# Two graph layers on one Trainium2 core: the order of work between layer 0 and the attention

## The chip, the cores and the metric

The kernel runs on one core of a Trainium2 chip. The metric is device time in microseconds (us) from start to end of one execution; three runs of the kernel before took 2220.85 to 2221.81, median 2221.29. A core has TensorE (matrix products), VectorE, ScalarE and GpSimd (called POOL in the profile), SyncE (SP), which issues most transfers, and DMA engines that carry them between the memory and the core. Each engine works through its own list of instructions in order, and instructions of different engines wait for each other where data or a buffer demands it.

## The reference

There are 3327 nodes with 1024 features, and an adjacency with about 1% of its entries filled. Layer 0 multiplies the adjacency with quantised features; layer 1 is an attention with 8 heads of 64, followed by a small network, each added to its input.

```python
# layer 0
h = relu(layernorm(x))
x = x + output            # adj @ support_q, scaled; support_q from h and the quantised weight
# layer 1
h = relu(layernorm(x))
Wh = einsum('nf,hfd->hnd', h, W)
e_src = einsum('hnd,hd->hn', Wh, a1); e_dst = einsum('hnd,hd->hn', Wh, a2)
e = leaky_relu(e_src[:, :, None] + e_dst[:, None, :], 0.2)
att = softmax(where(adj > 0, e, NEG))
h = elu(att @ Wh)         # heads side by side, then
x = x + mlp(h)            # 512 -> 256 -> 256 -> 512 -> 1024
```

The softmax is not computed entry by entry. The exponential of the leaky unit is one of two products, exp(src) exp(dst) or the same with slope 0.2, and which one holds depends on whether src > -dst. So the kernel keeps, for each node and head, its features times both exponentials ("features") and their difference, and multiplies them with two 0/1 matrices: the adjacency, and the adjacency where src > -dst.

## The kernel before

The nodes are padded to 26 tiles of 128 (`T = 26`). Each tile of columns is also a step `j` of the sums.

**Layer 0, second product (lines 711 to 757).** For each tile `t`, 104 products with 512 columns run in four parts (`SUBS`: 7, 6, 7 and 6 values of `j`), each `j` with an upper and a lower half of the adjacency (`hi`, `lo`) against `s_int[j]`. Then y is scaled on ScalarE and VectorE (L742, L744), added to the input (L745), written to `x1_d`, normalised (`normalised`, L137) and its inverse deviation `r` is formed (`half_inverse`: a root on ScalarE, reciprocals on VectorE). `transposed_by_dma` turns y: two copies on ScalarE (`yh`), two transposing transfers on SyncE's list (`yht`), two copies into `ht`. The last tile is turned by TensorE instead (`transposed_by_tensor`, two groups of four, both through one bank of `last_ps`).

**Heads (L630).** `heads(t)` forms Wh for a tile: eight products of `ht` with `whead` into `whm` (16 matmuls in the profile), then `wht` on ScalarE (called `taken`), on VectorE two products and two reductions for src and dst, the exponentials on ScalarE, two scalings `ft` on VectorE, and an upper half `fw` (ScalarE) and lower half `lows` (VectorE). POOL writes them to `feat_d` and `dsum_d` in memory. The src values are collected, turned by TensorE (`sp`) in the tiles named in `BATCHES` (12, 23 and 25) and written to `src_d` in rows. Heads of tile t - 1 stand before the last part of tile t's products; the last tile's stand after the loop, with `own` naming two tiles in the core (`f_even`, `dw`) that receive its values directly.

**Attention (L789 on).** `attends` has 32 entries of a half of the nodes, a head and one of two groups of row tiles. Each has 26 steps `n`. A step takes one selection `sel` on VectorE (L1057: one tile of columns for 7 or 6 row tiles, from `srow`, `ndst` and `mask`) and 7 or 6 products `acc` with `f_even` or `f_odd` (L1071). The four buffers of `sel` let VectorE run four steps ahead. In between stand products with the whole adjacency, called edges (L852, `mps<-dw,mf`): `mf` is the mask as numbers, cast on ScalarE in two halves, and `dw` the differences of features. `edge_steps(n)` says how many of them are due before step n: none until `FIRST`, then 12 a step up to `START` = 24, from `YOUNG` on in equal shares up to 338 at `LATE` = 62.

**The order around the change.** Order is written out by pins: `issue_after(a)` puts what is issued in its block behind `a` on the same engine, `queue_behind(a, b)` puts `a` behind `b`, without a wait of their own. Attention takes the memory of layer 0: `mask0` lies where `s_int` 0 to 6 were, `f_even` and `dw` where 6 to 19 were, `mask1` where 19 to 23 were, and each load waits until these were used last. SyncE's list before is: the transpositions of tile 24's y (`turned` is the second), xt of tile 25, `srow`, the first halves of seven masks, `f_even` for tiles 0 to 6, the masks' second halves, `f_even` and `dw` to tile 19, six masks of `mask1`, then `young`: `f_even` and `dw` for tiles 20 to 23, and for tile 24; `f_odd` after them. Steps 0 to 3 of the attention run while tile 25 is normalised, each of steps 4 to 11 ahead of one of the last heads' products.

Of the kernel before, what the change touches and what calls it, by code (L numbers as in the profile page):

```python
# [8 lines left out]
F32 = mybir.dt.float32  # L9
# [6 lines left out]
ALU = mybir.AluOpType  # L16
# [28 lines left out]
PARTS = SUBS  # L45
BATCHES = {12: 0, T - 3: 13, T - 1: T - 2}
GT = 2
# [14 lines left out]
def two_layer_kernel(  # L62
# [105 lines left out]
    with tc.tile_pool(name="at", bufs=2, reuse_waits="tile") as atp:  # L168
# [419 lines left out]
        with tc.tile_pool(name="wh", bufs=1, reuse_waits="tile") as whp, tc.tile_pool(  # L588
# [30 lines left out]

            def transposed_by_tensor(y):  # L620
                ht = s2.tile([P, KF, P], F32, name="ht", bufs=1)
                for g in range(KF // 4):
                    tp = last_ps.tile([P, 4, P], F32, tag="last", name="tp2")
                    for q in range(4):
                        k = 4 * g + q
                        nc.tensor.transpose(tp[:, q, :], y[:, k * P : (k + 1) * P], ident)
                    last = nc.scalar.copy(ht[:, 4 * g : 4 * g + 4, :], tp)
                return ht, last

            def heads(t, ht, r, own=None):  # L630
                if t == T - 1:
                    whm, sp = (last_ps.tile([P, EMB], F32, tag="last", name=n) for n in ("whm", "sp"))
                else:
                    whm = wh_ps.tile([P, EMB], F32, name="whm")
                    sp = sp_ps.tile([P, EMB], F32, name="sp")
                of_k, products = [], []
                for k in range(KF):
# [7 lines left out]
                ins = taken = nc.scalar.activation(wht, whm, AF.Copy, scale=r)  # L645
                if t < T - 1:
                    tc.keep_in_program_order(ins)
# [8 lines left out]
                nc.vector.tensor_scalar(ndst[:, t], dst, -1.0, None, ALU.mult)  # L656
                nc.scalar.activation(ratio[:, t], src, AF.Exp, scale=1.0 - SLOPE)
                if t in BATCHES:
                    first = BATCHES[t]
# [5 lines left out]
                    nc.scalar.copy(srct[:n], sp[:n, :P])  # L665
                    for u in range(first, t + 1):
                        d, sub = next((d, sub) for d, sub in zip(src_d, SUBS) if u in sub)
                        nc.gpsimd.dma_start(
                            d[:, (u - sub[0]) * P : (u - sub[0] + 1) * P],
                            srct[(u - first) * NH : (u - first + 1) * NH],  # L670
                        )

                ft = s2.tile([P, NH, 2, HC], F32, name="ft", bufs=1)
                wh3 = wht.rearrange("p (h d) -> p h d", d=HD)
                for q, slope in enumerate((1.0, SLOPE)):
                    exps = nc.scalar.activation(ft[:, :, q, HD], dst, AF.Exp, scale=slope)
                    scaled = nc.vector.tensor_tensor(  # L677
                        ft[:, :, q, :HD], wh3, ft[:, :, q, HD:].to_broadcast([P, NH, HD]), ALU.mult
                    )
                fw = s2.tile([P, NH, 2, 2 * HC], F32R, name="fw", bufs=1)  # L680
                f2 = ft.rearrange("p h q c -> p h (q c)")
                if own is not None:

                    parts = [dst[:, t].rearrange("p (q c) -> p q c", q=2) for dst in own]
                    ups = parts[0][:, 0], parts[1][:, 0].rearrange("p (e c) -> p e c", e=2)
                    downs = parts[0][:, 1], parts[1][:, 1].rearrange("p (e c) -> p e c", e=2)
                    values = f2[:, 0], ft[:, :2, 1]
                    for up, value in zip(ups, values):
                        nc.scalar.copy(up, value)
                    for up, down, value in zip(ups, downs, values):  # L690
                        scaled = nc.vector.tensor_tensor(down, value, up.bitcast(F32), ALU.subtract)
                nc.scalar.copy(fw[:, :, 0], f2)
# [15 lines left out]
                )  # L708
                return of_k, products, lows, exps, scaled, taken

            before = None
            for t in range(T):
# [27 lines left out]
                y = s2.tile([P, F], F32, name="y", bufs=1)  # L740
                with tc.issue_after(exps.ins) if t == T - 1 else nullcontext():
                    nc.scalar.activation(y, mm, AF.Copy, scale=r_asf)  # L742
                with tc.issue_after(made.ins) if t == T - 1 else nullcontext():
                    nc.vector.tensor_scalar(y, y, asf_t, sup_delta, ALU.mult, ALU.mult)  # L744
                nc.vector.tensor_tensor(xt, xt, y, ALU.add)  # L745
                nc.gpsimd.dma_start(x1_d[t * P : (t + 1) * P, :], xt)
                ln, v = normalised(y, xt)
                if t < T - 1:
                    ht, turned = transposed_by_dma(y)
                else:  # L750
                    ht, copied = transposed_by_tensor(y)

                with tc.issue_after(copied.ins) if t == T - 1 else nullcontext():
                    r = half_inverse(v, "ln")
                nc.vector.tensor_scalar(r, r, 2.0, None, ALU.mult)
                before = t, ht, r
            queue_behind(lows, ln)
            supp.close()
# [22 lines left out]
    EDGE = 13 * T  # L781
    FIRST = 12
    START = T - 2
    YOUNG = 14
    FRONT = 6
# [3 lines left out]
    with tc.tile_pool(name="srow0", bufs=1, reuse_waits="tile") as srow0, tc.tile_pool(  # L789
# [32 lines left out]
        def all_edges():  # L822

            for u, (c, g) in enumerate(units):
# [13 lines left out]
                for i in range(len(blocks)):  # L838
# [4 lines left out]
                    for j in range(T):  # L843
                        if j % TH == 0:
                            mf = (mf1 if j else mf0).tile([P, TH, P], F32R, tag="mf", name="mf")

                            amid = u == i == 0
                            with tc.issue_after(copied.ins) if amid else nullcontext():
                                ins = nc.scalar.copy(mf, mask[:, j : j + TH, :])  # L849
                            if amid:  # L850
                                queue_behind(taken, ins)
                        nc.tensor.matmul(ps, mf[:, j % TH, :], dw[:, j, :], start=(j == 0), stop=(j == T - 1))  # L852
                        if j == T - 1:
# [22 lines left out]

        mds = []
        edges = all_edges()
# [62 lines left out]

        old, young = PARTS[:3], [range(20, 24), range(24, 25)]
        with tc.issue_after(turned.ins):
            srow, ins = load_src(0)
        with tc.issue_after(ins.ins):
            ins = load_mask(0, SUBS[0], slice(0, TH))
        with tc.issue_after(ins.ins):
            load_features(f_even, feat_d, 0, old[:1])
            ins = load_mask(0, SUBS[0], slice(TH, T))
        with tc.issue_after(ins.ins):  # L950
# [3 lines left out]
            for js in young:  # L954
                load_features(f_even, feat_d, 0, [js])
                load_features(dw, dsum_d, 0, [js])
            load_features(f_odd, feat_d, 1, old + young + [range(T - 1, T)])
        for i, (c, g, e, si) in enumerate(attends):
# [82 lines left out]
            for j in range(T):  # L1041
# [12 lines left out]

                ahead = ln if j < 14 else scaled
                with tc.issue_after(ahead.ins) if i == 0 and j >= 4 else nullcontext():
                    ins = nc.vector.scalar_tensor_tensor(  # L1057
# [7 lines left out]
                if i == 0 and j < 4:  # L1065
                    queue_behind(products[0], ins)

                k = j - 4 if i == 0 and 4 <= j < 4 + KF else None
                with tc.issue_after(last_heads[k - 1].ins) if k else nullcontext():
                    for b in range(nb):  # L1070
                        ins = nc.tensor.matmul(  # L1071
                            accs[b], sel[:, b, :], f[:, j, :], start=(j == 0), stop=(j == T - 1)
                        )
# [126 lines left out]
```

## Time and profile before

| what | value |
|---|---|
| median of three runs | 2221.29 us |
| profiled execution, its own time | 2221.79 us |
| its span, first to last instruction | 2219.9 us |
| granted clock of TensorE, mean | 0.999 |
| last part of tile 25's products | 907.9 to 913.7 us |
| y of tile 25 normalised (L144 ends) | 920.0 us |
| heads' products of tile 25 | 923.2 to 935.6 us, between steps of attention |
| selection of step 14, first after tile 25's heads | 942.1 us |
| first attend ended (its sums copied) | 965.3 us on |

Times inside the kernel are given from the start of the span. A line of the timeline has start, duration, engine, line of the kernel, operation, what it writes and reads, the count of instructions merged, and in brackets how long the engine was idle before and what released it. One product with 512 columns appears as one instruction for layer 0 and as two for the heads. Durations of matmuls overlap; their spacing is what counts. The table of stretches gives, for each stretch, the busy time of each engine, then the granted clock, the mean share of the DMA engines and the data moved.

### The profile page before, as it was taken

To read this page: it belongs to the slowest core of one execution; us is meant where nothing else is said; L and a number is where in the kernel's file an instruction comes from. 1 tells how busy PE (TensorE), PEld (TensorE's weight loads), DVE (VectorE), ACT (ScalarE), POOL (GpSimd) and SP (SyncE) were. 2 spreads that over 40 slices of the span, in tenths; PEclk is the share of its full clock that TensorE was granted. 3 is DMA by queue.
4 is the path that set the end of the run, shared out by engine and by line. 5 is a ranking of instruction groups with operands and counts; after the bars stand their busy time and mean duration, and the time that the engine had idled before them with its cause. 6 is when DMAs were issued, how large, how long until landed. Compare 5 with 4: busy or idle time off the path is not lost.

```text
span 2219.9 us, 31285 instructions
## 1 busy us (share of the span) xinstructions
PE 2178.6 (98%) x12457; PEld 1748.6 (79%) x12457; DVE 1540.6 (69%) x1998; ACT 1113.6 (50%) x1714; POOL 176.0 (8%) x269
## 2 busy tenths in 40 slices
PE   5999999999999999999999999999999999999998
PEld 2477777777777777699999999999999999744444
DVE  8745555555455555678999999999999999732211
ACT  6734444544445544466555565555655555531220
POOL 2301000002000012000000000000000000000000
PEclk9999999999999999999999999999999999999999
DMA  6654566655655555934242422644242422383211
GB/s 218 164 185 155 158 189 181 179 165 156 183 184 184 170 168 157 331 116 149 87 149 78 142 90 73 222 143 149 83 149 87 140 87 78 102 208 114 104 57 57
DMA packets 242721, 321.40 MB, mean 145 GB/s; under 512 B 104900, under 2 KB 187284, under 8 KB 242576
## 3 DMA queue, kind: packets, MB, share of 16 engines
q1 hardware_dynamic: 222024, 246.24, 36.5%
q0 software_dynamic: 20544, 73.18, 10.5%
q8 instruction: 97, 1.59, 0.3%
q14 instruction: 48, 0.39, 0.1%
q10 hardware_dynamic: 8, 0.00, 0.0%
HBM read 208.99 MB, written 86.79 MB: 133 GB/s over the span
## 4 chain that ended last, share of the span: by engine, by line
PE 56%; DVE 1%; ACT 1%; issue 0%; DMA 0%; DVEq 0%
PE acc L1071 29%; PE mps L852 15%; PE o L1144 8%; PE h_ps L1107 4%; ACT enct L1129 0%; PE h_ps L1021 0%; PE whm L638 0%; DMA weights<-in_w1t 0%; DVE sel L1057 0%; ACT h L1114 0%; DVE nodes L1140 0%; DVE prod L652 0%; ACT su L896 0%; DVE ft L677 0%; DVE stats L141 0%
## 5 line engine op out<-in xcount | busy, mean ns | idle before, releaser
L1057 DVE SCALAR_TENSOR_TENSOR sel<-srow,ndst,mask 128x896 fp32r<-128x896 f32 (+1 forms) x832 | 864.8, 1082 | 52.3 <-PE acc L1071 40.1
L852 PE MATMUL mps<-dw,mf 128*128 128x260 f32 x2704 | 453.0, 283 | 0.3 <-ACT srct L665 0.3
L726 PE MATMUL mm<-s_int,hi 128*128 128x512 f32 x1352 | 426.7, 397 | 0.0
L726 PE MATMUL mm<-s_int,lo 128*128 128x512 f32 x1352 | 416.5, 389 | 0.0
L1071 PE MATMUL acc<-f_even,sel 128*128 128x260 f32 x2704 | 400.8, 286 | 3.1 <-DVE sel L1057 2.1
L1071 PE MATMUL acc<-f_odd,sel 128*128 128x260 f32 x2704 | 393.7, 286 | 1.1 <-ACT xs L1088 1.0
L849 ACT CAST mf<-mask 128x1664 fp32r<-128x1664 uint8 x208 | 331.4, 1594 | 118.8 <-PE mps L852 95.2
L852 PEld LDWEIGHTS mps<-dw,mf 128*128 128x128 f32 x2704 | 377.4, 188 | 1.1 <-ACT srct L665 0.6
L1071 PEld LDWEIGHTS acc<-f_even,sel 128*128 128x128 f32 x2704 | 356.8, 189 | 10.1 <-issue 3.6
L1071 PEld LDWEIGHTS acc<-f_odd,sel 128*128 128x128 f32 x2704 | 352.6, 188 | 8.4 <-issue 2.6
L726 PEld LDWEIGHTS mm<-s_int,hi 128*128 128x128 f32 x1352 | 254.0, 188 | 62.8 <-issue 12.0
L726 PEld LDWEIGHTS mm<-s_int,lo 128*128 128x128 f32 x1352 | 253.8, 188 | 52.7
L189 DVE TENSOR_TENSOR lo<-at,hi 128x896 fp32r<-128x896 f32 x104 | 106.2, 1021 | 132.4 <-ACT hi L185 132.2
L638 PE MATMUL whm<-whead,ht 128*128 128x512 f32 x416 | 183.8, 592 | 0.0
L1144 PE MATMUL o<-weights,h 128*128 128x512 f32 x416 | 179.7, 592 | 0.0
L190 DVE TENSOR_SCALAR mk<-at 128x896 uint8<-128x896 f32 (+1 forms) x104 | 61.5, 593 | 142.1 <-DMA at<-in_adj_t 142.1
L185 ACT CAST hi<-at 128x896 fp32r<-128x896 f32 x104 | 92.2, 886 | 135.4 <-PE mm L726 93.8
L1144 PEld LDWEIGHTS o<-weights,h 128*128 128x128 f32 x416 | 79.0, 190 | 99.1 <-issue 98.8
L638 PEld LDWEIGHTS whm<-whead,ht 128*128 128x128 f32 x416 | 78.3, 189 | 85.7 <-issue 83.8
L856 ACT COPY part<-mps 128x260 f32<-128x260 f32 x104 | 39.3, 378 | 188.2 <-PE mps L852 188.1
L1114 ACT ACTIVATE h<-h_ps,rest 128x512 f32<-128x512 f32 (+1 forms) x54 | 35.1, 653 | 194.2 <-PE h_ps L1107 194.2
L921 POOL DMA_DIRECT2D enc_d<-eh x64 | 57.5, 903 | 935.4 <-ACT eh L919 934.9
(166 smaller groups left out, 1666.6 us busy)
## 6 DMA issues: line engine op xcount, KB each, us to landing
feat_d<-fw POOLq DMA_DIRECT2D x26, 1040.0 KB, 5.3
f_even<-feat_d SPq DMA_DIRECT2D x7, 3380.0 KB, 13.5
f_odd<-feat_d SPq DMA_DIRECT2D x7, 3380.0 KB, 13.2
at<-in_adj_t SPq DMA_DIRECT2D x52, 448.0 KB, 4.3
at<-in_adj_t SPq DMA_DIRECT2D x52, 384.0 KB, 4.1
dw<-dsum_d SPq DMA_DIRECT2D x16, 910.0 KB, 9.0
dsum_d<-dw POOLq DMA_DIRECT2D x26, 520.0 KB, 6.3
x_d<-xt POOLq DMA_DIRECT2D x26, 512.0 KB, 6.7
```

The lines of the kernel that those rows point to most:

```text
L185: ins = nc.scalar.copy(hi, at)
L189: nc.vector.tensor_tensor(lo, at, hi.bitcast(F32), ALU.subtract)
L190: ins = nc.vector.tensor_scalar(mk[:, r], at, 0.0, None, ALU.is_gt)
L638: ins = nc.tensor.matmul(whm, ht[:, k, :], whead[:, k, :], start=(k == 0), stop=(k == KF - 1))
L726: nc.tensor.matmul(mm[:, c * 512 : (c + 1) * 512], which[:, q, :], s_int[j][:, c * 512 : (c + 1) * 512], start=(j == 0 and which is hi), s ...
L849: ins = nc.scalar.copy(mf, mask[:, j : j + TH, :])
L852: nc.tensor.matmul(ps, mf[:, j % TH, :], dw[:, j, :], start=(j == 0), stop=(j == T - 1))
L921: nc.gpsimd.dma_start(enc_d[q, sub[0] * P : (sub[-1] + 1) * P, h * HD : (h + 1) * HD].rearrange("(b p) d -> p b d", p=P), eh[:, q].rearran ...
L1057: ins = nc.vector.scalar_tensor_tensor(sel[:, :nb], srow[:, :nb], ndst[:, j, h : h + 1], mask[:, :, j, :], ALU.is_gt, ALU.mult,)
L1071: ins = nc.tensor.matmul(accs[b], sel[:, b, :], f[:, j, :], start=(j == 0), stop=(j == T - 1))
L1107: nc.tensor.matmul(ps[:, :cols], wt[:, k, m * P : (m + 1) * P], xt[:, k, :cols], start=(k == 0), stop=(k == k_n - 1),)
L1144: nc.tensor.matmul(ps[:, c * 512 : (c + 1) * 512], h3[:, k, q * P : (q + 1) * P], w4[:, k, c * 512 : (c + 1) * 512], start=(k == 0), stop= ...
```

## The change

- Tile 25 leaves `BATCHES`. The src values of tiles 24 and 25 are no longer turned; POOL writes each, 128 x 8 single numbers, straight to its places in `src_d`.
- `heads(24)` no longer stands before the last part of tile 25's products but behind them all, and stores its values also directly in `f_even` and `dw` (`own`). The loads of these for tile 24 are gone; `f_odd` loads tiles 24 and 25 one by one.
- `taken` and the first product of `heads(24)` stand behind the last operation of tile 25's deviation (`lacking`). The transpositions of tile 25 stand behind the products of `heads(24)`, the copies behind its `taken`, its exponentials behind the copies.
- Attention's step 0 stands between the two groups of transpositions, steps 1 to 3 between them and the heads of tile 25, steps 4 to 7 behind those heads, then 24 edges at once (`FIRST` 7, `YOUNG` 9), and step 8 behind them.
- On VectorE, selections 0 to 3 stand ahead of tile 25's scaling (`resumed`), 4 to 7 between tile 24's scalings and its lower halves, and from 8 on behind tile 25's scalings; tile 25's own lower halves follow selection 9 and `lows` selection 11.
- On SyncE, the first halves of the masks and `srow` are issued as soon as they may be, and tile 24's second transposition stands behind `srow`.
- The first casts `mf` stand behind tile 24's exponentials and ahead of tile 25's `taken`.

```diff
-BATCHES = {12: 0, T - 3: 13, T - 1: T - 2}
+BATCHES = {12: 0, T - 3: 13}
...
+                if t > max(BATCHES):
+                    with nc.allow_non_contiguous_dma(reason="two tiles' src values"):
+                        nc.gpsimd.dma_start(
+                            src_d[-1][:, (t - SUBS[-1][0]) * P : (t - SUBS[-1][0] + 1) * P].rearrange("h p -> p h"), src
+                        )
...
-                    if js is PARTS[-1] and before is not None:
-                        _, products, lows, exps, made, _ = heads(*before)
+                    if js is PARTS[-1] and before is not None and t < T - 1:
+                        heads(*before)
...
-            last_heads, *_, scaled, taken = heads(*before, own=(f_even, dw))
+            of_k, products, lows, powers, scaled, own_lows, taken = heads(*before, own=(f_even, dw))
+            queue_behind(products[0], lacking)
+            queue_behind(taken, lacking)
+            ht, turns, copies = transposed_by_tensor(y)
+            queue_behind(turns[0][0], of_k[-1])
+            queue_behind(copies[0], taken)
+            queue_behind(powers[0], copies[-1])
+            last = heads(T - 1, ht, r, own=(f_even, dw))
+            queue_behind(last[1][0], lows)
...
-    FIRST = 12
+    FIRST = 7
     START = T - 2
-    YOUNG = 14
+    YOUNG = 9
...
-                return min(max(0, n - FIRST) * 12, START)
+                return min(max(0, n - FIRST) * START, START)
...
-        old, young = PARTS[:3], [range(20, 24), range(24, 25)]
+        old, young = PARTS[:3], [range(20, 24)]
+        ins = load_mask(0, SUBS[0], slice(0, TH))
+        with tc.issue_after(ins.ins):
+            srow, ins = load_src(0)
+        queue_behind(turned, ins)
         with tc.issue_after(turned.ins):
-            srow, ins = load_src(0)
-        with tc.issue_after(ins.ins):
-            ins = load_mask(0, SUBS[0], slice(0, TH))
-        with tc.issue_after(ins.ins):
             load_features(f_even, feat_d, 0, old[:1])
...
-            load_features(f_odd, feat_d, 1, old + young + [range(T - 1, T)])
+            load_features(f_odd, feat_d, 1, old + young + [range(T - 2, T - 1), range(T - 1, T)])
...
+                    behind = tc.issue_after((scaled if j < 8 else last[4]).ins)
...
                 if i == 0 and j < 4:
-                    queue_behind(products[0], ins)
+                    queue_behind(resumed, ins)
+                elif i == 0 and j == 7:
+                    for later in (*own_lows, lows):
+                        queue_behind(later, ins)
+                elif i == 0 and j == 9:
+                    for later in last[5]:
+                        queue_behind(later, ins)
+                elif i == 0 and j == 11:
+                    queue_behind(last[2], ins)
+                behind = nullcontext()
+                if i == 0 and j <= 8:
+                    behind = tc.issue_after(
+                        (turns[0][1], *[turns[1][1]] * 3, *[last[0][-1]] * 4, *summed)[j].ins
+                    )
+                with behind:
                     for b in range(nb):
...
-                if k is not None:
-                    queue_behind(last_heads[k], ins)
+                if i == 0 and j in (0, 3):
+                    queue_behind(turns[1][0] if j == 0 else last[0][0], ins)
```

More of the change, by code (lines that the diff above doesn't have):

```diff
@@ L621, in transposed_by_tensor @@
                 ht = s2.tile([P, KF, P], F32, name="ht", bufs=1)
+                ends, copies = [], []
                 for g in range(KF // 4):
                     tp = last_ps.tile([P, 4, P], F32, tag="last", name="tp2")
[L624 to L628, printed above, removed]
+                    turns = [
+                        nc.tensor.transpose(tp[:, q, :], y[:, (4 * g + q) * P : (4 * g + q + 1) * P], ident)
+                        for q in range(4)
+                    ]
+                    ends.append((turns[0], turns[-1]))
+                    copies.append(nc.scalar.copy(ht[:, 4 * g : 4 * g + 4, :], tp))
+                return ht, ends, copies
             def heads(t, ht, r, own=None):
                 if t == T - 1:
-                    whm, sp = (last_ps.tile([P, EMB], F32, tag="last", name=n) for n in ("whm", "sp"))
+                    whm = last_ps.tile([P, EMB], F32, tag="last", name="whm")
                 else:
                     whm = wh_ps.tile([P, EMB], F32, name="whm")
-                    sp = sp_ps.tile([P, EMB], F32, name="sp")
-                of_k, products = [], []
+                of_k, products, own_lows = [], [], []
                 for k in range(KF):
@@ L645, in heads @@
                 ins = taken = nc.scalar.activation(wht, whm, AF.Copy, scale=r)
-                if t < T - 1:
+                if t < T - 2:
                     tc.keep_in_program_order(ins)
@@ L656, in heads @@
                 nc.vector.tensor_scalar(ndst[:, t], dst, -1.0, None, ALU.mult)
-                nc.scalar.activation(ratio[:, t], src, AF.Exp, scale=1.0 - SLOPE)
+                powers = [nc.scalar.activation(ratio[:, t], src, AF.Exp, scale=1.0 - SLOPE)]
                 if t in BATCHES:
+                    sp = sp_ps.tile([P, EMB], F32, name="sp")
                     first = BATCHES[t]
@@ L675, in heads @@
                 for q, slope in enumerate((1.0, SLOPE)):
-                    exps = nc.scalar.activation(ft[:, :, q, HD], dst, AF.Exp, scale=slope)
+                    powers.append(nc.scalar.activation(ft[:, :, q, HD], dst, AF.Exp, scale=slope))
                     scaled = nc.vector.tensor_tensor(
@@ L690, in heads @@
                     for up, down, value in zip(ups, downs, values):
-                        scaled = nc.vector.tensor_tensor(down, value, up.bitcast(F32), ALU.subtract)
+                        own_lows.append(nc.vector.tensor_tensor(down, value, up.bitcast(F32), ALU.subtract))
                 nc.scalar.copy(fw[:, :, 0], f2)
@@ L708, in heads @@
                 )
-                return of_k, products, lows, exps, scaled, taken
+                return of_k, products, lows, powers, scaled, own_lows, taken
             before = None
@@ L740, in two_layer_kernel @@
                 y = s2.tile([P, F], F32, name="y", bufs=1)
[L741 to L744, printed above, removed]
+                nc.scalar.activation(y, mm, AF.Copy, scale=r_asf)
+                resumed = nc.vector.tensor_scalar(y, y, asf_t, sup_delta, ALU.mult, ALU.mult)
                 nc.vector.tensor_tensor(xt, xt, y, ALU.add)
                 nc.gpsimd.dma_start(x1_d[t * P : (t + 1) * P, :], xt)
[L747 to L755, printed above, removed]
+                _, v = normalised(y, xt)
+                r = half_inverse(v, "ln")
+                lacking = nc.vector.tensor_scalar(r, r, 2.0, None, ALU.mult)
+                if t == T - 1:
+                    break
+                ht, turned = transposed_by_dma(y)
                 before = t, ht, r
-            queue_behind(lows, ln)
             supp.close()
@@ L847, in all_edges @@
                             amid = u == i == 0
-                            with tc.issue_after(copied.ins) if amid else nullcontext():
+                            with tc.issue_after(powers[-1].ins) if amid else nullcontext():
                                 ins = nc.scalar.copy(mf, mask[:, j : j + TH, :])
                             if amid:
-                                queue_behind(taken, ins)
-                        nc.tensor.matmul(ps, mf[:, j % TH, :], dw[:, j, :], start=(j == 0), stop=(j == T - 1))
+                                queue_behind(last[-1], ins)
+                        summed[:] = [
+                            nc.tensor.matmul(ps, mf[:, j % TH, :], dw[:, j, :], start=(j == 0), stop=(j == T - 1))
+                        ]
                         if j == T - 1:
@@ L875, in edge_steps @@
             return EDGE * (u + 1) + first + min(rest, EDGE - T)
-        mds = []
+        mds, summed = [], []
         edges = all_edges()
@@ L1053, in two_layer_kernel @@
                 sel = selp.tile([P, 7, P], F32R, tag="sel", name="sel")
-                ahead = ln if j < 14 else scaled
-                with tc.issue_after(ahead.ins) if i == 0 and j >= 4 else nullcontext():
+                behind = nullcontext()
+                if i == 0 and j >= 4:
+                    behind = tc.issue_after((scaled if j < 8 else last[4]).ins)
+                with behind:
                     ins = nc.vector.scalar_tensor_tensor(
@@ L1065, in two_layer_kernel @@
                 if i == 0 and j < 4:
-                    queue_behind(products[0], ins)
-                k = j - 4 if i == 0 and 4 <= j < 4 + KF else None
-                with tc.issue_after(last_heads[k - 1].ins) if k else nullcontext():
+                    queue_behind(resumed, ins)
[7 more added lines that the diff above has]
+                    queue_behind(last[2], ins)
+                behind = nullcontext()
+                if i == 0 and j <= 8:
+                    behind = tc.issue_after(
+                        (turns[0][1], *[turns[1][1]] * 3, *[last[0][-1]] * 4, *summed)[j].ins
+                    )
+                with behind:
                     for b in range(nb):
```

## The prediction

> **What bounds the kernel now.** I read the page first, then the chain of waits, then TensorE's timeline from 900 to 970 us, then a table of 4 us stretches, and last what SyncE issued.
>
> ```profile
> span 2219.9 us, 31285 instructions
> PE 2178.6 (98%) x12457; PEld 1748.6 (79%) x12457; DVE 1540.6 (69%) x1998; ACT 1113.6 (50%) x1714; POOL 176.0 (8%) x269
> ```
>
> TensorE is busy for 98%, so only its gaps can be won. All that the change touches lies between 883 and 966 us, where layer 0 turns into attention. TensorE's timeline there (start, us, what, idle before it):
>
> ```profile
> 913.71 0.64 PE L1071 MATMUL acc<-f_even,sel 128*128 128x260 f32 x4
> 915.39 2.56 PE L1071 MATMUL acc<-f_even,sel 128*128 128x260 f32 x19 [1.04 <-ACT y L742]
> 920.02 0.66 PE L626 MATMUL tp<-ident,y 128*128 128x128 f32 x4 [2.07 <-DVE y L144]
> ...
> 939.07 3.58 PE L852 MATMUL mps<-dw,mf 128*128 128x260 f32 x26 [0.34 <-ACT srct L665]
> 943.32 1.11 PE L1071 MATMUL acc<-f_even,sel 128*128 128x260 f32 x7 [0.68 <-DVE sel L1057]
> 945.53 6.83 PE L1071 MATMUL acc<-f_even,sel 128*128 128x260 f32 x42 [1.11 <-DVE sel L1057]
> ```
>
> The reader should see three holes: two while tile 25's rows are normalised (1.04 and 2.07), and a thin stretch from 938 to 945.5 while tile 25's heads pass ScalarE and VectorE. The stretches show what else is full (us, busy PE, PEld, DVE, ACT, POOL, clock, DMA share, GB/s):
>
> ```profile
> 886.00:890.00 4.00, 4.00 (x19) 3.34 (x18) 3.86 (x7) 1.55 (x3) 2.56 (x4) 1.00 0.54 177
> 890.00:894.00 4.00, 4.00 (x19) 3.30 (x19) 1.52 (x3) 3.78 (x5) 0.00 (x0) 1.00 1.01 343
> 894.00:898.00 4.00, 4.00 (x20) 3.30 (x19) 0.70 (x4) 0.95 (x2) 0.00 (x0) 1.00 1.20 184
> 898.00:902.00 4.00, 4.00 (x18) 3.18 (x17) 0.96 (x1) 2.34 (x3) 0.00 (x0) 1.00 0.89 244
> 902.00:906.00 4.00, 4.00 (x10) 1.72 (x10) 0.00 (x0) 0.00 (x0) 0.00 (x0) 1.00 1.02 381
> ...
> 934.00:938.00 4.00, 3.81 (x25) 2.88 (x23) 1.07 (x2) 1.81 (x2) 0.00 (x0) 1.00 1.05 389
> 938.00:942.00 4.00, 3.20 (x25) 3.02 (x26) 3.45 (x8) 1.58 (x8) 1.06 (x2) 1.00 0.79 266
> 942.00:946.00 4.00, 2.22 (x14) 1.68 (x14) 4.00 (x5) 4.00 (x5) 1.27 (x2) 0.99 0.13 14
> 946.00:950.00 4.00, 4.00 (x23) 4.00 (x22) 4.00 (x5) 1.12 (x2) 0.45 (x1) 0.59 0.91 251
> ```
>
> The DMA engines are full from 890 to about 941 without a break. And after the thin stretch the clock falls to 0.59 for 4 us, which costs some 1.7 us. What SyncE sent among its last before 940, and (size, us to landing) the answer on DMA issues for the middle one:
>
> ```profile
> 917.29 6.13 SPq L809 DMA_DIRECT2D mask<-mask_d x6
> 924.91 0.37 SPq L805 DMA_DIRECT2D f_even<-feat_d x1
> 931.48 0.37 SPq L805 DMA_DIRECT2D dw<-dsum_d x1
> ```
>
> ```profile
> f_even<-feat_d SPq DMA_DIRECT2D x1, 520.0 KB, 14.1
> ```
>
> f_even's tiles 20 to 23 land at 924.91 + 14.1 = 939.0. dw's tiles 20 to 23, 0.53 MB, stand right behind them: at 0.36 MB/us they land 1.4 us later, at 940.4. The edge product of tile 20 runs at 939.07 + 20 x 0.12 = 941.5. So before, this transfer is just in time, and no wait shows it.
>
> **What the Trainium skill says.** "TensorE: Matmul & The Clock Gate", Part 1, says that an idle window of about 3.4 us halves the clock until a busy window has passed; the trace agrees (0.59 in 946:950). Part 2 of that page says that matmuls stay in program order; so one that waits holds up all behind it. "DMA: Bandwidth & Descriptors", Queues, rings and completion order, says that a DMA engine takes turns between queues packet by packet; the trace agrees in kind: POOL's write of x_d, issued at 917.9, landed in 6.3 us, while SyncE's six masks of the same moment, behind SyncE's earlier ones, took 14.2 (median).
>
> **The change, part by part** (times on the clock of the profiled execution; matmul spacing from the timeline: layer 0 0.227 us, heads 0.43, attention and edges 0.12, a transposition 0.11).
>
> *Tile 24's heads behind the last product.* The last 24 products start at 901.4 and end at 906.8, not 913.7. The heads' 16 matmuls (6.9 us) then run to 913.7. Beside them tile 25's chain: y on ScalarE 1.1, then VectorE's scaling, addition, statistics and subtraction 4.5 (915.5 to 920.0 in the trace), so done at about 912.6. Both holes go: -3.1. The cover is the 6.9 us; without it the chain would cost 5.7. The pin puts VectorE's scaling behind selections 0 to 3 (4 x 1.07), and behind it waits all of VectorE and the transpositions. These selections started at 906.88 when the mask landed; they need it by some 904. The masks may now go when tile 25's products with s_int 0 to 6, whose place they take, are done: 901.4 - 13 x 0.91 = 889.6, so I take landing at 898 to 901: hidden.
>
> *Masks and srow ahead of the second transposition of tile 24.* Seven masks and srow, 1.95 MB, 5.4 us at 0.36, pass in front; behind it on SyncE wait also xt and f_even. ht came at 900.3 and would come at up to 905.7; it is wanted at 906.8. Hidden, with 1 us left. ScalarE's last hi stands between the two copies of ht; if it is held it delays the last products by 0 to 3 us. Below I show that there is slack behind, so I take 0.
>
> *Order up to the edges.* TensorE from 913.7: transpositions 0.9, step 0 0.84, steps 1 to 3 2.5, tile 25's heads 6.9, steps 4 to 7 3.4; with 0.5 for small waits 928.7. On ScalarE the pins give root, wht of tile 24 (914.0 to 914.7; step 0's fifth sum takes its bank), two copies of ht (1.2), the table load 1.28 and the exponentials; it has nothing else that is due. VectorE: tile 24's products, reductions and scalings 914.7 to 919.5, selections 4 to 7 to 923.8, ahead of the end of the heads (925.3). Tile 25's chain then ends at about 930 behind steps 4 to 7 and the edges. So far all holes are closed.
>
> *The 24 edges* come after step 7: tile 20 is wanted at 928.7 + 2.4 = 931.1, not 941.5. Step 8 is pinned behind tile 23, and everything on TensorE is behind step 8. So the question is when dw's tiles 20 to 23 land.
>
> *The DMA ledger.* In front of them stand the same transfers as before: mask halves 2 x 1.49, srow 0.46, xt 0.52, f_even 3.46 + 0.53, dw 2.66, mask1 2.56, x_d 0.52, tile 23's writes; 17.3 MB had moved from 886 to 938 (the sum of the stretches), always at share 0.89 or more since 890. To issue the masks 8 us earlier fills no idle engine; it puts them in front of the transpositions, which come later. Only tile 24's own writes (feat_d 1.06 and dsum_d 0.53 MB, 4.4 us) can leave the list. They were issued at 921.4. Now VectorE's lows follow selection 7 and end at 925.5, so POOL issues them at 925.6. Some 9 us of SyncE's list are left then, and the writes, in packets four times as large, take turns with it: I let nearly all of them get in front. Taken out are tile 24's and 25's rows of src by one transposition (two DMAs of 4 KB); added are two writes of 1024 elements of 4 bytes. No row shows such a write. From below, 896 pieces of enc_d cost POOL 0.9 us and I take 1 us of POOL, which is idle; on the DMA engines 0 to 3.5 us each (enc_d's 896 pieces landed in 3.1), and I take 0.5 for the one in front. Landing: 940.4 + 0.5 - 0.4 for the writes' tail = 940.5, from 936.0 (all writes behind) to 944 (both src writes dear). TensorE so stands from 931.1 to 940.5.
>
> *After that.* I compare at one amount of work. Before had done 26 steps and 95 edges at 964.9. The new order has 8 steps and 20 edges at 940.5; 18 x 0.84 + 75 x 0.12 = 24.1 are left. The standstill of 9 us halves the clock; half of the time until a whole busy window has passed is lost: 1.0 to 2.7, taken 1.9. 940.5 + 24.1 + 1.9 = 966.5, against 964.9: +1.6. VectorE is ahead by four selections then and hides. From 966 to 1022 TensorE has no gap and step 62 finds the same count of edges in both formulas (338), so +1.6 stays to the end. Tile 24 straight from its heads saves two small loads behind this point: nothing.
>
> The profiled execution took 2221.79 us, 1.9 more than its span; the median is 2221.29. The span goes to 2221.5, that run to 2223.4, the median to 2222.9.
>
> **Rivals.** *The tiles land in time.* If SyncE gets the young tiles out ahead of mask1 (2.56 MB, 7 us), they land at 933.5, the stand is 2.4 us and no clock is lost: 957.6, -7.3, so 2214. For it: the young tiles' place is free earlier than mask1's. Against it: before has mask1 in front. Full cover would give 931.1 + 24.1 = 955.2, -9.7: the most there is.
>
> *Slower: the small src writes are dear.* With 3.5 us each in front of dw the tiles land at 944 and, with two clock windows (2.7), 970.8: +5.9, so 2227. It decides from a landing at 943.3. For it: 4-byte pieces. Against it: 4 KB only. A late hi would show here only if it moved the edges past 940.
>
> *The writes come last*: landing 936.0, clock 1.5: -3.3, 2218; within the likeliest case's range.
>
> **How the numbers follow.** Likeliest (landing 936 to 943): 0.61, 2218 to 2225.5. In time: 0.14. Late: 0.25. A measurement tells about 0.2%, 4.4 us, from no change; so faster 0.14, same 0.61, slower 0.25. The range leaves a tenth on each side: 2216 to 2227.5.
>
> **What would show it.** Right: no idle on TensorE from 901 to 928 above 0.5 us; a wait of mps for DMA dw of 6 to 10 us from about 931; a clock near 0.6 for 3 us behind it; full DMA stretches from 890 to 940; selections 4 to 7 done before tile 25's heads. Wrong: dw's tiles landed by 932, the young tiles issued ahead of mask1, or a wait of the last layer 0 products for hi above 1 us.

## The result and the profile after

| kernel | median, us | runs | ratio to before, 95% interval |
|---|---|---|---|
| before | 2221.55 (2220.85 to 2223.14) | 4 | |
| after | 2244.62 (2243.21 to 2245.83) | 4 | 1.0106 [1.0094, 1.0118] |

The change makes the kernel about 1% slower, 23 us, far outside the predicted range of 2216 to 2227.5. The page of the kernel after, its span, its engines and its costliest group of edges (busy us, mean ns | idle before, and what ended it):

```profile
span 2243.1 us, 31272 instructions
...
PE 2179.8 (97%) x12446; PEld 1750.8 (78%) x12456; DVE 1542.2 (69%) x2000; ACT 1111.3 (50%) x1713; POOL 176.7 (8%) x269
...
L865 PE MATMUL mps<-dw,mf 128*128 128x260 f32 x2704 | 457.0, 284 | 27.1 <-DMA dw<-dsum_d 27.1
```

TensorE does the same work (2179.8 us busy, 2178.6 before), and the span is 23.2 us longer. The edges now stand for 27.1 us, all of it for the load of dw. TensorE's timeline in the kernel after says which edges:

```profile
907.99 7.03 PE L641 MATMUL whm<-whead,ht 128*128 128x512 f32 x16
914.86 0.60 PE L627 MATMUL tp<-ident,y 128*128 128x128 f32 x4
...
919.33 7.03 PE L641 MATMUL whm<-whead,ht 128*128 128x512 f32 x16
925.79 3.92 PE L1100 MATMUL acc<-f_even,sel 128*128 128x260 f32 x28
929.55 1.00 PE L865 MATMUL mps<-dw,mf 128*128 128x260 f32 x7
933.35 1.67 PE L865 MATMUL mps<-dw,mf 128*128 128x260 f32 x6 [2.80 <-DMA dw<-dsum_d]
935.55 1.88 PE L865 MATMUL mps<-dw,mf 128*128 128x260 f32 x7 [0.53 <-DMA dw<-dsum_d]
961.17 1.24 PE L865 MATMUL mps<-dw,mf 128*128 128x260 f32 x4 [23.74 <-DMA dw<-dsum_d]
```

Up to 930 no line has a bracket: heads of tile 24, transpositions, steps 0 to 3, heads of tile 25 and steps 4 to 7 follow each other without a hole, as intended. Then the edges of tiles 7 to 12 and 13 to 19 wait 2.80 and 0.53 us, and those of tiles 20 to 23 wait 23.74 us: dw's tiles 20 to 23 come at 961.1, where the prediction had 940.5. The table of stretches (columns as before: busy time of PE, PEld, DVE, ACT, POOL, then clock, DMA share, GB/s) shows where the transfer's time went:

```profile
918.00:922.00 4.00, 4.00 (x20) 2.56 (x19) 3.54 (x6) 3.99 (x8) 0.39 (x1) 1.00 1.09 358
922.00:926.00 4.00, 4.00 (x12) 1.80 (x10) 4.00 (x6) 2.16 (x3) 0.00 (x0) 1.00 1.30 110
926.00:930.00 4.00, 4.00 (x33) 3.81 (x32) 2.61 (x5) 1.43 (x3) 2.29 (x3) 1.00 1.15 40
...
938.00:942.00 4.00, 0.00 (x0) 0.00 (x0) 1.63 (x3) 1.06 (x1) 0.00 (x0) 0.50 1.04 398
942.00:946.00 4.00, 0.00 (x0) 0.00 (x0) 1.10 (x1) 0.11 (x1) 0.89 (x1) 0.50 1.51 132
946.00:950.00 4.00, 0.00 (x0) 0.00 (x0) 0.00 (x0) 1.04 (x2) 0.76 (x1) 0.50 0.80 48
950.00:954.00 4.00, 0.00 (x0) 0.00 (x0) 0.00 (x0) 0.00 (x0) 0.00 (x0) 0.50 1.08 285
```

Read the last two columns together. The DMA engines are as "busy" as ever, but twice, for some 8 us, they move 40 to 130 GB/s instead of 360 to 400. A share of 1 at a tenth of the rate means packets that take long, not many packets: the trace has 1377 packets of 1040 bytes from 918 to 922, and 152 from 926 to 930. Two dips, and two small writes of src values. POOL's timeline and, below it, the answers on DMA issues for the two writes (size, us to landing) and for before's writes of the same tensor in rows:

```profile
917.49 0.91 POOL L678 DMA_DIRECT2D src_d<-srcs  x1 [5.11 <-DVE srcs L656]
...
929.37 0.90 POOL L678 DMA_DIRECT2D src_d<-srcs  x1 [1.04 <-DVE srcs L656]
```

```profile
src_d<-srcs POOLq DMA_DIRECT2D x1, 4.0 KB, 15.7
...
src_d<-srcs POOLq DMA_DIRECT2D x1, 4.0 KB, 21.9
```

```profile
src_d<-srct POOLq DMA_DIRECT2D x13, 4.0 KB, 1.5
```

The same 4 KB land in 1.5 us (the median of 13; 2.9 for the two of tiles 24 and 25) as 8 rows of 512 bytes, and in 15.7 and 21.9 us as 1024 single numbers. The engines were not equally full in these cases, so the landing times alone prove nothing yet. 917.49 + 15.7 is 933.2 and 929.37 + 21.9 is 951.3: the dips lie inside these spans.

### The profile page after: what moved, and what is told of

Read it like the earlier page. It is cut to its first block, busy times and chain, and to the rows that moved or that the text cites. A ratio compares the mean times of both kernels' runs of the same rounds, so it can differ in the third digit from the quotient of the medians.

```text
span 2243.1 us, 31272 instructions
## 1 busy us (share of the span) xinstructions
PE 2179.8 (97%) x12446; PEld 1750.8 (78%) x12456; DVE 1542.2 (69%) x2000; ACT 1111.3 (50%) x1713; POOL 176.7 (8%) x269
## 3 DMA queue, kind: packets, MB, share of 16 engines
q0 software_dynamic: 20544, 73.18, 10.4%
## 4 chain that ended last, share of the span: by engine, by line
PE 85%; DMA 6%; DVE 3%; ACT 2%; issue 1%; SPq 1%; POOL 0%; DVEq 0%; ACTq 0%; POOLq 0%
PE acc L1100 29%; PE mm L735 22%; PE mps L865 14%; PE o L1173 7%; PE whm L641 6%; PE h_ps L1136 4%; PE mm L337 2%; DMA dw<-dsum_d 2%; DMA at<-in_adj_t 1%; DMA yht<-yh 1%; DMA xqt<-xq 0%; DMA nodes<-x_d 0%; DVE lo L189 0%; ACT enct L1158 0%; DMA mask<-mask_d 0%
## 5 line engine op out<-in xcount | busy, mean ns | idle before, releaser
L865 PE MATMUL mps<-dw,mf 128*128 128x260 f32 x2704 | 457.0, 284 | 27.1 <-DMA dw<-dsum_d 27.1
```

## The experiments

My theory after this result: the two small writes take the DMA engines' time, and the rest of the prediction's sum holds. The rival: dw's tiles come late because of the order itself (tile 24's large writes, mask1 and the rest ahead of them), and the small writes only land late because everything does. Medians of before within the series are 2220.96 to 2221.65; each ratio is to the runs of before in the same series.

**e1: both small writes moved.** They go behind the first attend's writes of `enc_d`; nothing reads these values before the second half of the row tiles needs them. Instructions and order of all other engines stay.

```diff
-                if t > max(BATCHES):
-                    ...
-                        nc.gpsimd.dma_start(src_d[-1][...].rearrange("h p -> p h"), src)
...
-                nc.gpsimd.dma_start(
+                ins = nc.gpsimd.dma_start(
...
+            if i == 0:
+                for t in (T - 2, T - 1):
+                    with tc.issue_after(ins.ins), ...:
+                        nc.gpsimd.dma_start(src_d[-1][...].rearrange("h p -> p h"), srcs[:, t])
```

> The changed kernel, with the two writes of src for tiles 24 and 25 moved behind the first attend's writes of enc_d (about 1010 us); every other engine's list is unchanged. Theory A (these two writes of 1024 elements of 4 bytes hold up the DMA engines for some 8 us each): the wait of the edges for dw shrinks from 27 us to about 10, the tiles 20 to 23 of dw land near 942 instead of 961, and the time is 2221 to 2226 us. Theory B (the new order of the loads, with masks ahead of the transposition and tile 24's features written later, delays dw): the wait stays over 20 us and the time at 2240 to 2246.

2223.47 us, ratio 1.0012 [1.0005, 1.0019]. TensorE's timeline and two of its stretches in e1:

```profile
941.64 1.23 PE L860 MATMUL mps<-dw,mf 128*128 128x260 f32 x4 [9.93 <-DMA dw<-dsum_d]
```

```profile
922.00:926.00 4.00, 4.00 (x12) 1.85 (x11) 3.96 (x6) 1.77 (x3) 0.00 (x0) 1.00 1.09 361
926.00:930.00 4.00, 4.00 (x36) 4.00 (x35) 2.65 (x4) 1.43 (x3) 1.67 (x2) 1.00 1.03 399
```

No dip, and 21.2 of the 23.1 us are gone. What is left is the wait that the prediction named: from 931.7 to 941.6. That is as the first theory expected.

**e2: only tile 25's write moved**, by the same edit.

> The changed kernel with only tile 25's write of src moved to about 1010 us; tile 24's stays at 917. Theory A: half of the extra wait goes, time 2230 to 2236, and one of the two dips of the DMA rate (that of 942 to 950) is gone. Theory B: 2240 to 2246.

2229.85 us (four runs, 2227.80 to 2236.69), ratio 1.0047 [1.0030, 1.0064], just under the 2230 to 2236 expected; one dip, 922 to 930 at 72 and 97 GB/s, and the restart:

```profile
946.64 1.23 PE L865 MATMUL mps<-dw,mf 128*128 128x260 f32 x4 [12.29 <-DMA dw<-dsum_d]
```

So tile 24's write costs 5.0 us of landing and, by the medians, 6.4 us of time (e2 less e1; with so wide a spread of e2 good to a few us). Tile 25's costs 14.5 us of landing (961.17 less 946.64) and 14.8 us of time: more, though its pieces are the same.

**e3: the kernel before with the small writes** instead of the transposition of tiles 24 and 25, its order kept.

```diff
-BATCHES = {12: 0, T - 3: 13, T - 1: T - 2}
+BATCHES = {12: 0, T - 3: 13}
...
+                if t > max(BATCHES):
+                    ...
+                        nc.gpsimd.dma_start(src_d[-1][...].rearrange("h p -> p h"), src)
```

> The kernel before, with the src values of tiles 24 and 25 written straight as 1024 elements of 4 bytes instead of by the transposition on TensorE; nothing else of the change. Theory A: tile 24's write comes at about 912, in front of most of dw, and the edges wait for dw by 6 to 10 us: time 2227 to 2232; tile 25's comes behind dw and costs the edges nothing. Theory B: no wait for dw, time 2219 to 2223.

2235.98 us, ratio 1.0066 [1.0051, 1.0081]. The edges, which did not wait for `dw` before, now show

```profile
959.78 1.67 PE L858 MATMUL mps<-dw,mf 128*128 128x260 f32 x6 [18.61 <-DMA dw<-dsum_d]
```

with dips from 918 to 926 (101 and 112 GB/s) and from 946 to 954 (56 and 168). It is more than the 2227 to 2232 expected: as the second dip shows, once the first write had delayed dw, the second stood in front of it too. The writes cost some 15 us in before's order, and without them the new order costs 2 (e1): the rival falls.

**e8 and e7: the young tiles first.** On SyncE, f_even's and dw's tiles 20 to 23 (in e7 to 24) go ahead of mask1's six loads; e8 on the kernel after with its small writes in place, e7 on the kernel before as a control.

```diff
-            load_mask(1, SUBS[1])
             for js in young:
                 load_features(f_even, feat_d, 0, [js])
                 load_features(dw, dsum_d, 0, [js])
+            load_mask(1, SUBS[1])
```

> The kernel after, its two small writes where the change puts them, but the young tiles ahead of mask1 on SyncE. dw's tiles then have 2.56 MB (7 us) less in front of them and the second small write, issued at 929.4, comes too late to stand in front: dw should land at 937 to 945 instead of 961.1, TensorE wait 6 to 14 us instead of 27, and the time be 2222 to 2230 us. If both small writes cost their full price still, dw lands at about 953 and the time stays above 2234.

> A control: the kernel before with f_even's and dw's tiles 20 to 24 loaded ahead of mask1. It did not wait for dw, so my theory says no difference: 2219 to 2223 us. If to load the young tiles first is a gain by itself, whatever the order on TensorE, it shows here as 2217 to 2218.

e8 took 2230.16 us, ratio 1.0039 [1.0026, 1.0053], just above the upper end of what I expected, and dw's tiles came at 947.4, later than the 937 to 945 expected. TensorE's timeline and two stretches of e8:

```profile
947.46 1.23 PE L865 MATMUL mps<-dw,mf 128*128 128x260 f32 x4 [11.72 <-DMA dw<-dsum_d]
```

```profile
922.00:926.00 4.00, 4.00 (x21) 2.63 (x20) 2.71 (x5) 1.50 (x3) 1.22 (x2) 1.00 1.01 27
...
938.00:942.00 4.00, 0.00 (x0) 0.00 (x0) 1.24 (x1) 1.06 (x1) 0.89 (x1) 0.50 1.18 66
```

Both dips are there: I was wrong that the second write would come too late to stand in front; it ran while dw's last tiles were still on their way. e7 took 2220.43 us, ratio 0.9999 [0.9990, 1.0007]: before did not wait for dw, so it gains nothing.

**e5: small writes late and young tiles first.** The edits of e1 and e8 together.

> The changed kernel with late writes of src and, on SyncE, f_even and dw of tiles 20 to 23 ahead of the six masks of mask1 (2.56 MB). Theory A with a transfer queue that is full from 890 on: dw lands about 7 us earlier than with late writes alone, near 935, the wait is 3 to 4 us, no clock is lost and the time is 2213 to 2217. If another transfer than the small writes held dw, it stays above 2230.

2218.40 us, ratio 0.9986 [0.9980, 0.9993]: faster than before by a little, but short of the 2213 to 2217 expected. TensorE waits for dw no more: the tiles land at 929.1, earlier than expected. Its largest hole left there, the VectorE line that fills it and the ScalarE line behind that one, from three timelines of e5:

```profile
938.07 6.42 PE L1102 MATMUL acc<-f_even,sel 128*128 128x260 f32 x42 [2.21 <-DVE sel L1077]
```

```profile
935.71 1.24 DVE L697 TENSOR_TENSOR fw<-ft,fw 128x1040 fp32r<-128x1040 f32 x1 [1.00 <-ACT fw L696]
```

```profile
934.62 1.06 ACT L696 CAST fw<-ft 128x1040 fp32r<-128x1040 f32 x1 [3.36 <-DMA feat_d<-fw]
```

The one buffer of `fw` is free only when tile 24's features are in memory. Tile 25's upper half waits for that, its `lows` waits for the upper half, and selection 12 stands behind `lows` by the pin of the change.

**e9: e5 with that pin moved** from selection 11 to 13.

> e5 (small writes late, young tiles first) with tile 25's lower halves (lows) behind selection 13 instead of 11. VectorE no longer waits for the write of tile 24's features to free fw: the hole of 2.21 us at 938 on TensorE should shrink to 1.4 or less, but selections at 1.1 us a step still pace TensorE (0.84 us a step) up to the next edges: 2214.5 to 2218.5 us, 0 to 2 below e5 (2218.4). If the hole only moves: same as e5 within 1 us.

2217.78 us, ratio 0.9985 [0.9977, 0.9993]. VectorE's wait is gone (`lows` at 939.79 without a bracket), and the hole is smaller:

```profile
942.15 6.43 PE L1102 MATMUL acc<-f_even,sel 128*128 128x260 f32 x42 [1.13 <-DVE sel L1077]
```

Between e9 and e5 the times cannot be told apart. Up to the next edges VectorE's 1.08 us a selection paces TensorE, whose step is 0.84, so a hole closed early comes back as short waits.

**e6, e10, e12: what makes the pieces dear.** To e1, spare writes of tile 25's src values are added in quiet stretches of the attention, to memory that nothing reads; they differ in size, number and spacing of the pieces, and in the engine that issues them. Each of the three ran once: 2224.10, 2226.26 and 2227.34 us, the last just above the 2222 to 2227 expected. The edit of e12, shortened:

```diff
+            if i in (1, 3, 4, 5):
+                c = {1: 2, 3: 4, 4: 8, 5: 1}[i]
+                with tc.issue_after(ins.ins), ...:
+                    nc.gpsimd.dma_start(pieces[...].rearrange("(h p c) -> p h c", p=P, c=c)[:, :, 0], srcs[:, T - 1])
```

> The kernel of e1 with four writes of tile 25's src values added in quiet stretches of the attention, to a spare place in memory that nothing reads: from POOL 128 pieces of 32 bytes (about 1040 us), 512 of 8 bytes (about 1091) and 1024 of 4 bytes (about 1124), and from SyncE 1024 of 4 bytes (after 1224). All carry the same 4 KB. If the price goes with the number of pieces, they land in about 2.5, 7, 13.5 and 13 us; if it is the size of the piece (anything that small is dear), the first three all take 8 us or more; if it is POOL's queue that makes the 4-byte pieces slow, SyncE's lands in under 4 us. TensorE waits for none of them directly: 2222 to 2227 us.

> e6 left open why 1024 pieces of 4 bytes take 10.9 us and 512 of 8 bytes 4.1, both from POOL. The kernel of e1 with four other spare writes from POOL, of values nothing reads: 512 pieces of 4 bytes side by side (about 1039 us), 1024 of 8 bytes side by side (1091), 1024 of 4 bytes each 64 bytes from the next (1124), 1024 of 4 bytes each 512 bytes from the next (1162). If the number of pieces sets it above some hundreds, they take 4, 11, 11 and 11 us; if pieces of 4 bytes are dear as such, 7, 5, 11 and 11; if it is that many pieces meet in the same few bytes of memory, 7 or more, 7 or more, and 4 for each of the spread ones. Time 2222 to 2227 us.

> The kernel of e1 with four spare writes of 1024 pieces of 4 bytes from POOL in quiet stretches, to a place that nothing reads: 8 bytes from piece to piece (about 1040 us), 16 (1091), 32 (1124), and side by side (1162). From e10 the last should take 10 to 14 us. If pieces hinder each other only inside the same 8 bytes (e6 and e10: pieces of 8 bytes side by side took 4 to 5), the first three take 3 to 5 us; if inside a longer line of 32 or 64 bytes, the first two or three take 6 us or more. Time 2222 to 2227 us.

Issue to landing, us; where the answer on DMA issues gives none, it is the last count of the transfer's semaphore in the trace less the start of the issue ("at least" where counts are missing from the trace):

| pieces | from one to the next | from | us |
|---|---|---|---|
| 128 of 32 B | side by side | POOL (e6) | 3.7 |
| 512 of 8 B | side by side | POOL (e6) | 4.1 |
| 1024 of 8 B | side by side | POOL (e10) | 4.5 |
| 512 of 4 B | side by side | POOL (e10) | 10.1 |
| 1024 of 4 B | side by side | POOL (e6, e12) | at least 10.9, at least 10.4 |
| 1024 of 4 B | side by side | SyncE (e6) | 11.6 |
| 1024 of 4 B | 8 B | POOL (e12) | 5.3 |
| 1024 of 4 B | 16, 32 B | POOL (e12) | 3.7, 3.7 |
| 1024 of 4 B | 64, 512 B | POOL (e10) | 3.4, 3.0 |

Two of these in the answers on DMA issues of e10 (512 pieces side by side with the larger writes ahead of them, then 1024 pieces 64 bytes apart with theirs):

```profile
enc_d<-eh POOLq DMA_DIRECT2D x2, 96.0 KB, 6.7
pieces<-srcs POOLq DMA_DIRECT2D x1, 2.0 KB, 10.1
```

```profile
enc_d<-eh POOLq DMA_DIRECT2D x2, 112.0 KB, 3.0
pieces<-srcs POOLq DMA_DIRECT2D x1, 4.0 KB, 3.4
```

None of e6's three theories fits. It is not the number: 1024 pieces of 8 bytes take 4.5 us. It is not the size: 1024 pieces of 4 bytes, 64 apart, take 3.4. It is not POOL's queue: SyncE's took 11.6. Dear are only pieces of 4 bytes right beside each other, which here come from neighbouring partitions. Of e10's three theories the last comes nearest: it missed only the 8-byte pieces. The larger writes just ahead landed late as well: 6.7 us, against 3.0 and 2.6 ahead of the pieces 64 and 512 bytes apart. Ahead of the 8-byte pieces it was 5.7 us, but there one of the 16 counts of each write's semaphore came late, and ahead of the 512 pieces ten of the second write's. e12's first row, 5.3 us at 8 bytes, is a little over what I expected.

**e11: spread pieces at the critical place.** e1, and where the kernel after has its small writes, two writes of the same 1024 values with 64 bytes from piece to piece, to memory that nothing reads.

```diff
                 if t > max(BATCHES):
                     ...
                         nc.gpsimd.dma_start(
-                            src_d[-1][...].rearrange("h p -> p h"), src
+                            pieces[t - T].rearrange("(h p c) -> p h c", p=P, c=16)[:, :, 0], src
```

> The kernel of e1, with two more writes exactly where the kernel after has its two small ones: the same 1024 values of tiles 24 and 25, in pieces of 4 bytes, from POOL, but each piece 64 bytes from the next, to a place that nothing reads. If the dip of the DMA engines comes from pieces that stand side by side in memory, nothing much happens: dw lands at 941 to 945, TensorE waits 10 to 14 us, 2222.5 to 2227 us. If any 1024 pieces from POOL do it, it is the kernel after again: dw at 955 or later, above 2236 us.

2227.69 us, ratio 1.0027 [1.0017, 1.0037]: 17 us below the kernel after, 0.7 above my upper end. Stretches and restart of e11:

```profile
922.00:926.00 4.00, 4.00 (x12) 1.84 (x10) 4.00 (x6) 2.27 (x3) 0.00 (x0) 1.00 1.11 309
926.00:930.00 4.00, 4.00 (x33) 3.76 (x32) 2.61 (x5) 1.43 (x3) 2.18 (x3) 1.00 1.04 399
```

```profile
943.34 1.24 PE L866 MATMUL mps<-dw,mf 128*128 128x260 f32 x4 [11.13 <-DMA dw<-dsum_d]
```

The dips are gone with the same values, pieces, queue and moments; only the place in memory and the spacing differ, and e6 and e12 show that side by side the pieces land late in a spare place too. So the packing of the pieces is shown to be the cause of the dips. The spread writes themselves still landed after 7.0 and 11.4 us among the other transfers. The restart is 1.7 us behind e1's; the rest of the 4.2 us between the two comes after it, and I did not follow it.

## Why the prediction was wrong

One line of the DMA ledger failed: the price of the small writes and how many of them stand in front of dw's tiles. The other steps held within about 1 us. Point by point:

*Tile 24's heads behind the last product; transpositions; order up to the edges:* right. The two holes of 1.04 and 2.07 us are gone, and the edges begin at 929.55 where the prediction had 928.7; all of the kernel after runs about 1 us later than before already ahead of the change's place.

*Masks and srow in front of the second transposition:* right. The heads of tile 24 start at 907.99 without a wait, and no product of layer 0 waits for `hi`.

*Selections 4 to 7 ahead of the end of tile 25's heads, tile 24's writes:* right. Steps 4 to 7 follow the heads without a bracket; POOL issues tile 24's features at 926.67 (925.6 was predicted).

*The 24 edges wait for dw's tiles 20 to 23:* the mechanism and the place are right (the smaller waits of 2.80 and 0.53 us belong to the first dip; e1 has none), and e1, whose only difference is the small writes, took 2223.47 us against the predicted 2222.9. So masks, edges and clock loss were sized well enough (in e1 dw's tiles came 1.1 us later than predicted, and the clock, at 0.65 from 942 to 946, cost 1.6 us where 1.9 was taken).

*The DMA ledger, the small writes: "0 to 3.5 us each (enc_d's 896 pieces landed in 3.1), and I take 0.5 for the one in front":* here the prediction failed, twice in one line.

First the price. The 896 pieces of `enc_d` that bounded it are 128 bytes long. The pieces of src are 4 bytes, side by side. From 922 to 930 e1 moved (361 + 399) x 4 = 3.04 MB (GB/s times us is KB) and the kernel after (110 + 40) x 4 = 0.60: 2.44 MB less, at 0.36 MB/us 6.8 us. From 942 to 954, against 360 GB/s, (228 + 312 + 75) x 4 = 2.46 MB less: again 6.8 us.

Second, "the one in front". With dw due at 940.5, the second write, issued at 929.4, could be left out of the sum. With the first write dear, dw's tiles slipped, and then the second stood in front as well. So did tile 25's own writes of features, 1.6 MB or 4.4 us, issued at 943.39 and 947.33 and landed by 961. 6.8 + 6.8 + 4.4 = 18.0 of the 19.5 us by which the restart is later than e1's. This is an estimate: e2 has the first write alone, and its restart is 5.0 us later than e1's, not 6.8, so some 3 us are not assigned.

*After that:* the sum holds with the right landing. Restart 961.17, plus the 24.1 us of work that the prediction counted from there, plus half of the 5.5 us for which the clock stays at 0.50 behind the restart (the stretch 962 to 966 shows 0.50, the next 0.91, so it ends near 966.7), 2.76 (1.9 was taken), is 988.0 against 964.9: +23.1, and the spans differ by 23.2.

"TensorE: Matmul & The Clock Gate", Part 1, in the Trainium skill, says that the full clock comes back only after a busy window of about 3.4 us; the 5.5 us fit a window that began some 2 us behind the restart. The idle window that the prediction cites from the same part fits before's trace less well: ahead of the 0.59 at 946, TensorE was still busy for 2.22 of the 4 us from 942 to 946.

*The rival "the small src writes are dear"* had the right mechanism. It priced each write at 3.5 us, counted one in the landing, and so ended at 2227, 18 us short. *The rival "in time"* (2214) needed the young tiles ahead of mask1; e8 and e5 show that this order alone is not enough (2230.16), and that with the small writes away it reaches 2218.4: the wait for dw goes, but VectorE, which the rival left out, then paces TensorE.

## What to carry to other kernels

When a DMA writes single 4-byte numbers next to each other in memory, turn them first (before's transposition made rows of 512 bytes, 1.5 us) or leave room between them (no run here reads such spread values back), and until then keep the write away from a stretch in which the DMA engines are full. A bound taken from a neighbouring row is good only for the same size and layout of pieces; where neither is in the trace, the upper end must be asked for what it sets off: here a transfer that slipped let what was issued meanwhile get in front of it. In a table of stretches, a DMA share of 1 beside a rate of a tenth was the sign of such a write; a half rate was not: the stretch of before from 894 to 898 has 184 GB/s at a share of 1.20 without one.

## What the runs showed of the hardware

Pieces of 4 bytes side by side took 10.1 us for 512 and at least 10.4 for 1024 (11.6 from SyncE), with 3.0 to 3.7 us for the same 1024 when 16 bytes or more lay between their starts. "DMA: Bandwidth & Descriptors", Specifications, in the Trainium skill says that transfers under 512 bytes are done by reading, changing and writing back. That may be what happens here, but size alone is not the price: 8-byte pieces side by side cost 4.1 to 4.5 us. That several pieces must fall into the same 8 bytes fits the rows of the table, with 5.3 us at a spacing of 8 bytes still a little dear; why it is slow no run shows.

Such a write also holds up the other queue. The same page, Queues, rings and completion order, says that an engine takes turns between queues by packet; in the kernel after, single packets of 1040 bytes of SyncE's queue, 47 ns as a rule, took up to 4.9 us while the pieces ran, and in e1 from 922 to 930 at most 0.14 us. So taking turns did not keep SyncE's queue moving here. It shows on engines with little else to do as well: SyncE's load of `srow`, issued 2.1 us behind the write, landed after 12.5 us beside e12's pieces side by side, and after 4.1 us beside e10's pieces 512 bytes apart.
